# A graph layer with routed experts: 192 instead of 256 slots for each expert of the third group

## The chip, the cores and the metric

The kernel runs on one core of one Trainium2 chip, all in float32. The metric is the device time of a run in microseconds, the median of several runs; lower is better. Before the change it is 1236.64 us.

## The reference, cut to what matters

The input is 3,125 nodes of 256 features and 100,000 directed edges, sorted by their target. The layer adds a graph part and an attention part to the nodes, then a mixture of 8 experts of which each node uses its best two:

```python
xn = _layernorm(x, axis=-1)
x = x + gnn(xn, src, dst, theta, phi) + mix(xn[None], w_qkv, w_out, b_out)[0]
x = x + ffn(_layernorm(x)[None], Wr, br, ln_g, ln_b, W1, b1, W2, b2)[0]
...
# gnn: the largest message over a node's incoming edges
e = relu((x[dst] - x[src]) @ theta.T + x[src] @ phi.T)
out = segment_max(e, dst)
...
# ffn: E = 8 experts, D = 256, H = 1024
probs = softmax(xt @ Wr + br);  top_p, top_idx = top_k(probs, 2)
weights = top_p / top_p.sum(-1)
h = gelu(einsum('end,edh->enh', xn * ln_g + ln_b, W1) + b1)
y = einsum('enh,ehd->end', h, W2) + b2
out = sum over the two of weights * y[top_idx]
```

## The kernel before, in words

**Nodes and groups.** The nodes lie in 25 tiles of 128. Most edges end at the first nodes, so the edges are taken from the last target to the first, and the tiles in four groups as their edges are done: tiles 12 to 24, 6 to 11, 1 to 5, and tile 0 (`GROUPS`, line 41, with `STEPS`, line 42, the columns of 128 edges of each). What is left of the edges is handled apart.

**Edges.** GpSimd gathers one row of `b_d` for each of 128 edges per instruction (helper `gather`, line 106), into windows of 8 steps out of a pool of 5 buffers named `g`. VectorE folds each step into a running maximum (`fold`, line 365), SyncE's queue stores the windows to `s_d`. When a group's steps are folded, its tiles are routed (`token_tile`, lines 421 to 494): the last row of each node is gathered from `s_d`, joined with what other lanes carried over, normalized, and the router's two best experts are taken.

**Slots.** In the first three groups each node's row is scattered by GpSimd into `xs_d`, which has a fixed number of slots for each expert: `CAPS`, line 43, is 512, 256 and 256 for the three groups. `slots` (line 518) counts the rows of each expert; if one has more rows than slots, a flag in `bad` sends the program into a general path at its end (line 1393).

**The experts of the three groups** run as a stream of lots (`Stream`, line 652). A lot is 256 rows of one expert; two lots (`two`, line 664) are loaded with one transfer on ScalarE's queue. `turn` (line 683) transposes a lot on TensorE, `scaled` (line 692) applies the expert's gain and bias on ScalarE. `Units.run` (line 606) then makes 8 steps. In each, line 613 multiplies 128 hidden columns of W1 (stationary) with the lot's rows (moving, 256 columns) in two halves, line 615 applies the gelu, and `second` (line 624) makes an eighth of the second layer of the lot *before*: at line 639 hT is the stationary operand, in parts of 128 rows, and W2's 256 columns move. `done` (line 738) adds the second bias with a matmul (line 740), copies the part to `ys` (line 741), and stores two lots at a time to `ys_d`. A float32 matmul is two instructions in the trace. The weights of an expert are 2 MB, in three buffers, loaded in parts on ScalarE's queue between the steps.

**Tile 0**, the last, is not scattered: all its rows go through all 8 experts (`dense_tile`, line 773), in the order of `DENSE` (line 35), with the same `Units` at 128 rows. It starts with three experts' weights left by the stream; the others are loaded during it, one of them by `dense_half` (line 1181) into two buffers of the pool `g` (line 1310) after the routing of tile 0 (`clock["shared"]`, line 1136).

**Combining.** `combine` (line 1277) gathers each node's two rows from `ys_d`, weights and adds them on VectorE (line 1290), and stores tiles to `out` on SyncE's queue. These start after the last edge gather; the sums wait for `shared`.

**What orders the work.** TensorE, VectorE, ScalarE and SyncE run in an order written out by the program: tasks are generators that yield a number of ticks (`start`, `tick`, lines 1049 to 1066). A tick stands for 1.25 us (`TICK`, line 57), and each gather or scatter on GpSimd moves the clock on by one. `on_pe` (line 78) charges TensorE work to a second clock, and `room` (line 648) makes the stream yield until that clock is no more than two ticks ahead; so the charges decide how many steps of the experts are put between other work. In the dense layer a step yields one tick, and it doesn't start before the stream is through (line 792, set at line 764).

Of the kernel before, what the change touches and what calls it, by code (L numbers as in the profile page):

```python
# [13 lines left out]
AF = mybir.ActivationFunctionType  # L14
# [5 lines left out]
P = 128  # L20
# [4 lines left out]
D = 256  # L25
# [5 lines left out]
E = 8  # L31
H = 1024
FC = H // P
# [6 lines left out]

GROUPS = ((12, 25), (6, 12), (1, 6), (0, 1))
STEPS = (240, 161, 228, 126)
CAPS = (512, 256, 256)
G = len(GROUPS)
COL = [sum(STEPS[:g]) for g in range(G + 1)]

# [11 lines left out]
ROWS = 256  # L58
# [8 lines left out]
def gps_layer(ctx: ExitStack, tc: tile.TileContext, x, src, dst, thetaT, phiT, gbias, wq, wkvT,  # L67
              woT, bout, wr, br, small, w12, b2, out):
    nc = tc.nc
# [8 lines left out]
    def on_pe(us):  # L78
        clock["pe"] = max(clock["pe"], clock["now"]) + us / TICK
# [46 lines left out]
    ident = keep.tile([P, P], F32, name="ident")  # L126
# [472 lines left out]
    class Units:  # L599

        def __init__(self, ps, act, n, whole=False):
            self.ps, self.act, self.n, self.behind, self.whole = ps, act, n, None, whole

        def run(self, e, w1t, xe, w2t, done, between):

            n = self.n
            hT = []
            for f in range(FC):  # L610
                hp = self.ps.tile([P, ROWS], F32, name="hp")
                for c in range(2):
                    nc.tensor.matmul(hp[:, 0:n], w1t[:, c, f, :], xe[:, c, 0:n], start=(c == 0), stop=(c == 1))  # L613
                hT.append(self.act.tile([P, ROWS], F32, name="hT", bufs=14))
                nc.scalar.activation(hT[f][:, 0:n], hp[:, 0:n], AF.Gelu, bias=sm[:, 4 + f, e:e + 1])  # L615
                on_pe(n / P * 0.43)
                self.second(f)
                if f in between:
                    between[f]()
                yield  # L620
            self.second(FC)
            self.behind = [hT, w2t, done, {}]

        def second(self, f):

            if self.behind is None:
                return
            hT, w2t, done, yp = self.behind
            ns = self.n // P
            per = FC * ns // FC  # L630
            if f and f * per % FC == 0:
                done(f * per // FC - 1, yp[f * per // FC - 1])
            if f == FC:
                return
            for k in range(f * per, (f + 1) * per):
                r, q = k // FC, k % FC
                if q == 0:
                    yp[r] = self.ps.tile([P, D], F32, name="yp")
                nc.tensor.matmul(yp[r], hT[q][:, r * P:(r + 1) * P], w2t[:, q, :], start=(q == 0),  # L639
                                 stop=(q == FC - 1 and self.whole))  # L640
            on_pe(per * 0.43)

# [9 lines left out]
    class Stream:  # L652
# [18 lines left out]
        def at(self, to):  # L671

            return xn_hi[:, 4 * to:4 * to + 4, :]

        def as_two(self, rows, v):
            return rows.rearrange("p (k s) d -> p k s d", k=1 if CAPS[self.lots[2 * v][0]] == 2 * ROWS else 2)

        def rows(self, v):
            if 2 * v < len(self.lots) and ("xs", v) not in self.held:
# [3 lines left out]
        def turn(self, u):  # L683
            if ("xs", u // 2) in self.held and ("tr", u) not in self.held:
                tr = self.held["tr", u] = self.ps.tile([P, 2, ROWS], F32, name="trf", bufs=1)
                for c in range(2):
                    for r in range(ROWS // P):
                        nc.tensor.transpose(tr[:, c, r * P:(r + 1) * P],  # L688
                                            self.held["xs", u // 2][:, u % 2 * 2 + r, c * P:(c + 1) * P], ident)
                on_pe(ROWS / P * 0.6)  # L690

        def scaled(self, u):
            if ("tr", u) in self.held and ("xe", u) not in self.held:
                e = self.lots[u][1]
                xe = self.held["xe", u] = self.act.tile([P, 2, ROWS], F32, name="xe")
                for c in range(2):
                    nc.scalar.activation(xe[:, c, :], self.held["tr", u][:, c, :], AF.Identity,
                                         bias=sm[:, 2 + c, e:e + 1], scale=sm[:, c, e:e + 1])

        def next_w(self, q, parts=None):  # L700
# [5 lines left out]
                self.parts.pop(0)()  # L706

        def go(self):
            units = Units(self.ps, self.act, ROWS)
            u, q = 0, -1  # L710
            for k in range(3):
                self.next_w(k)
                yield 25
            while True:
                if u == len(self.lots):

                    for _ in units.last():
                        yield room()
                    units.behind = None
                    if not self.open:  # L720
                        break
# [12 lines left out]
                v = u // 2  # L734
                if u % 2 == 0:
                    ys = self.at(2) if v % 2 else self.act.tile([P, 4, D], F32, name="ys", bufs=1)

                def done(r, yp, u=u, ys=ys):
                    g, e, h = self.lots[u]
                    nc.tensor.matmul(yp, ident[0:E, e:e + 1].to_broadcast([E, P]), b2_sb, start=False, stop=True)  # L740
# [17 lines left out]
                for _ in units.run(e, w1t, self.held["xe", u], w2t, done, between):  # L758
# [14 lines left out]
    def dense_tile(act, ps, mm, i, shared, w, next_w, order=range(E), ready=None):  # L773
# [7 lines left out]
        held = {}  # L781
# [28 lines left out]
        units = Units(ps, act, P, True)  # L810
        for k, e in enumerate(order):
            def done(r, yp, k=k, e=e):
                if k == 0:
                    nc.vector.tensor_scalar(o, yp, full[:, e:e + 1], None, op0=OP.mult)
                else:
                    nc.vector.scalar_tensor_tensor(o, yp, full[:, e:e + 1], o, op0=OP.mult, op1=OP.add)

            between = {1: lambda k=k: scaled(k + 1)}
            if k == 1:
                between.update({3: second_bias, 5: add_bias})  # L820
            if k > 1:
                between[1] = lambda k=k: (next_w(k - 2), scaled(k + 1))
            while k == 1 and not shared:
                yield 1
            for _ in units.run(e, w[e][0], held["xe", e], w[e][1], done, between):
                yield 1
        nc.vector.tensor_add(o, o, x_sb[:, i, :])
        for _ in units.last():
# [49 lines left out]
    def loads():  # L878
# [664 lines left out]
```

## Time and profile before

| | |
|---|---|
| median of 3 runs | 1236.64 us (1230.59 to 1245.63) |
| the profiled execution's own time | 1752.15 us |
| its span, first to last instruction | 1750.4 us |
| TensorE matmul busy | 1035.4 us |
| VectorE busy | 670.9 us |
| ScalarE busy | 330.2 us |
| GpSimd busy | 881.0 us |
| mean granted TensorE clock | 0.756 of full |
| moved by DMA | 322.09 MB |

The profiled execution is 515.5 us longer than the median of the runs. A profile line of a group gives its line, engine, operation, tiles and count, then its busy time with the mean duration of one, then the idle time of the engine ahead of it and what ended that. In order of time, a line gives its start and duration in us, engine, line and count. "PEld" is TensorE's weight load. Matmul durations overlap, so that the distance of their starts is their pace. In the table by stretches each engine has its busy time and its count of instructions; the last columns are the granted TensorE clock, the share in which the 16 DMA engines were busy, and what they moved.

### The profile page before, as it was taken

What the parts mean: (1) busy time and instruction counts of PE and PEld (TensorE: products, weight loads), DVE (VectorE), ACT (ScalarE), POOL (GpSimd) and SP (SyncE); (2) the same over time, 40 slices, a digit from 0 to 9 for tenths busy, and PEclk for the clock granted to TensorE, in tenths of its full rate; (3) what the DMA queues carried; (4) which work ended last, traced back from release to release, by engine and by line L of the source; (5) the groups of instructions that cost most, each with busy time, mean ns of one, the idle gap of its engine ahead of it and who ended that gap; (6) DMA issues with size and microseconds to landing.
All of it is one profiled execution on the core that took longest, in us unless ns stands there. A gap on an engine that the chain in (4) does not pass through costs nothing.

```text
span 1750.4 us, 13366 instructions
## 1 busy us (share of the span) xinstructions
PE 1035.4 (59%) x3931; PEld 726.5 (42%) x3931; DVE 670.9 (38%) x1989; ACT 330.2 (19%) x763; POOL 881.0 (50%) x911
## 2 busy tenths in 40 slices
PE   3633654533653574169678735669677424299886
PEld 2412322321222332048556623457456213178675
DVE  3635554674254532310046440251253453013332
ACT  1301121110121211013123201213122111032232
POOL 6374757557556437723541573552462747723332
PEclk7866877866675577569887866889889556599998
DMA  7454756556465226416554563566687438468282
GB/s 230 133 160 158 235 198 199 192 189 220 146 234 186 107 92 215 151 53 219 183 173 154 188 206 99 181 230 235 229 276 248 148 136 285 122 207 298 69 288 89
DMA packets 105292, 322.09 MB, mean 184 GB/s; under 512 B 20982, under 2 KB 44911, under 8 KB 93690
## 3 DMA queue, kind: packets, MB, share of 16 engines
q0 software_dynamic: 44032, 119.73, 22.7%
q1 hardware_dynamic: 29740, 115.08, 16.9%
q10 hardware_dynamic: 31438, 86.33, 14.9%
q8 instruction: 33, 0.54, 0.1%
q14 instruction: 49, 0.40, 0.1%
HBM read 192.71 MB, written 128.36 MB: 183 GB/s over the span
## 4 chain that ended last, share of the span: by engine, by line
PE 40%; another core or an unknown queue 25%; issue 17%; DVE 11%; ACT 3%; DMA 3%; POOL 1%; ACTq 0%; DVEq 0%; SPq 0%; POOLq 0%
PE hp L613 15%; PE yp L639 13%; DVE g L365 4%; PE yp L740 2%; PE mm L402 2%; PE kv L998 1%; PE bp L240 1%; PE mm L400 1%; ACT hT L615 1%; POOL g L106 1%; PE trf L688 1%; DMA g<-b_d,srcI 1%; ACT sq L1002 1%; DVE r L449 1%
## 5 line engine op out<-in xcount | busy, mean ns | idle before, releaser
L106 POOL DMA_INDIRECT g<-b_d,srcI x755 | 733.9, 972 | 531.7 <-DMA s_d<-g 224.1
L613 PE MATMUL hp<-xe,w 128*128 128x256 f32 (+1 forms) x1216 | 334.1, 403 | 288.1 <-issue 180.4
L365 DVE SCALAR_TENSOR_TENSOR g<-g,cut 128x256 f32<-128x256 f32 x751 | 362.4, 483 | 247.0 <-DMA g<-b_d,srcI 146.2
L613 PEld LDWEIGHTS hp<-xe,w 128*128 128x128 f32 x1216 | 236.1, 210 | 349.2 <-issue 201.5
L639 PE MATMUL yp<-w,hT 128*128 128x256 f32 x1120 | 313.7, 405 | 0.0
L615 ACT ACTIVATE hT<-hp,sm 128x256 f32<-128x256 f32 (+1 forms) x320 | 143.7, 452 | 672.0 <-PE hp L613 274.8
L639 PEld LDWEIGHTS yp<-w,hT 128*128 128x128 f32 x1120 | 221.5, 203 | 43.5 <-issue 12.6
L1213 DVE SCALAR_TENSOR_TENSOR xn_lo<-xn_lo,no_edge 128x256 f32<-128x256 f32 x96 | 46.0, 480 | 194.9 <-DMA xn_lo<-b_d 178.2
L998 PE MATMUL kv<-wkv,xn_lo 128*128 128x512 f32 x96 | 61.0, 795 | 89.9 <-DVE kn L1016 39.7
L998 PE MATMUL kv<-wkv,xn_hi 128*128 128x512 f32 x104 | 59.7, 727 | 65.9 <-DVE kn L1016 37.1
L106 POOL DMA_INDIRECT g<-ys_d,from_i x48 | 45.5, 947 | 73.1 <-DMA out<-g 46.2
L106 POOL DMA_INDIRECT r<-s_d,end_i x25 | 24.1, 964 | 101.8 <-DMA s_d<-g 63.0
L998 PEld LDWEIGHTS kv<-wkv,xn_lo 128*128 128x128 f32 x96 | 23.5, 257 | 119.3 <-issue 99.4
L400 PE MATMUL mm<-bias,ones 1*128 1x512 f32 x50 | 36.0, 807 | 60.9 <-ACT x_sb L407 47.1
L998 PEld LDWEIGHTS kv<-wkv,xn_hi 128*128 128x128 f32 x104 | 23.3, 236 | 93.4 <-issue 91.2
L113 POOL DMA_INDIRECT xs_d<-xn_lo,slot_i x22 | 22.6, 1027 | 73.4 <-issue 62.6
L444 PE MATMUL am<-cr,oh 128*128 128x257 f32 x88 | 38.4, 567 | 29.2 <-DVE r L449 15.8
L113 POOL DMA_INDIRECT xs_d<-xn_hi,slot_i x26 | 27.3, 1050 | 50.4 <-issue 50.1
L1007 DVE TENSOR_REDUCE var<-sq 128x16 f32<-128x1024 f32 x25 | 30.4, 1215 | 47.3 <-ACT sq L1002 25.3
L740 PE MATMUL yp<-b_sb,ident 8*128 8x256 f32 x128 | 46.5, 444 | 0.0
L488 PE MATMUL mm<-br_sb,ones 1*128 1x8 f32 x50 | 12.9, 329 | 55.8 <-issue 37.6
L1002 ACT ACTIVATE sq<-kv 128x1024 f32<-128x1024 f32 x25 | 25.5, 1019 | 103.6 <-PE kv L998 44.6
(285 smaller groups left out, 999.6 us busy)
## 6 DMA issues: line engine op xcount, KB each, us to landing
s_d<-g SPq DMA_DIRECT2D x80, 1024.0 KB
w<-in_w ACTq DMA_DIRECT2D x84, 512.0 KB
w<-in_w ACTq DMA_DIRECT2D x6, 2048.0 KB
g<-b_d,srcI POOLq DMA_INDIRECT x755
s_d<-g SPq DMA_DIRECT2D x13, 896.0 KB
xn_hi<-xs_d ACTq DMA_DIRECT2D x16, 512.0 KB
xs_d<-zero ACTq DMA_DIRECT2D x8, 512.0 KB
xs_d<-zero ACTq DMA_DIRECT2D x16, 256.0 KB
```

The source lines that it names most:

```text
L106: got = nc.gpsimd.indirect_dma_start(out=to, out_offset=None, in_=table, in_offset=row_index(index))
L113: put.append(nc.gpsimd.indirect_dma_start(out=table, out_offset=row_index(index), in_=of, in_offset=None))
L365: nc.vector.scalar_tensor_tensor(g[:, j, :], last, cut[:, t:t + 1], g[:, j, :], op0=OP.add, op1=OP.max)
L400: nc.tensor.matmul(am, ones[0:1, :], bias, start=True, stop=False)
L444: nc.tensor.matmul(r2, picks[k], carried[g], start=(k == 0), stop=(k == len(slices) - 1))
L613: nc.tensor.matmul(hp[:, 0:n], w1t[:, c, f, :], xe[:, c, 0:n], start=(c == 0), stop=(c == 1))
L615: nc.scalar.activation(hT[f][:, 0:n], hp[:, 0:n], AF.Gelu, bias=sm[:, 4 + f, e:e + 1])
L639: nc.tensor.matmul(yp[r], hT[q][:, r * P:(r + 1) * P], w2t[:, q, :], start=(q == 0), stop=(q == FC - 1 and self.whole))
L740: nc.tensor.matmul(yp, ident[0:E, e:e + 1].to_broadcast([E, P]), b2_sb, start=False, stop=True)
L998: nc.tensor.matmul(kv[:, k, :], xnT(i, c), wkv[:, c, k * INNER:(k + 1) * INNER], start=(c == 0), stop=(c == 1))
L1002: nc.scalar.activation(sq, kv.rearrange("p k (h e) -> p (k h) e", e=DH), AF.Square)
L1213: nc.vector.scalar_tensor_tensor(of_k[:, k, :], b, no_edge[:, k, i:i + 1], of_k[:, k, :], op0=OP.add, op1=OP.max)
```

## The change

The third group gets 192 slots for each expert, and its lots have 192 rows in two parts of 96 instead of two of 128. For that, `Units` takes the number of parts and their rows with each run, and the transfers, transposes, scalings, bias matmuls and copies of a lot cover the rows that it has. A pair of lots of the third group lies on 96 partitions. The lots of the other groups, and tile 0, have the rows that they had.

```diff
-CAPS = (512, 256, 256)
+CAPS = (512, 256, 192)
+LOT = (256, 256, 192)
...
-        def run(self, e, w1t, xe, w2t, done, between):
-
-            n = self.n
+        def run(self, e, w1t, xe, w2t, done, between, parts, part):
+
+
+            n = parts * part
             hT = []
             for f in range(FC):
                 hp = self.ps.tile([P, ROWS], F32, name="hp")
...
-            self.behind = [hT, w2t, done, {}]
+            self.behind = [hT, w2t, done, {}, parts, part]
...
-            hT, w2t, done, yp = self.behind
-            ns = self.n // P
-            per = FC * ns // FC
+            hT, w2t, done, yp, per, part = self.behind
...
-                nc.tensor.matmul(yp[r], hT[q][:, r * P:(r + 1) * P], w2t[:, q, :], start=(q == 0),
+                nc.tensor.matmul(yp[r][0:part, :], hT[q][:, r * part:(r + 1) * part], w2t[:, q, :], start=(q == 0),
                                  stop=(q == FC - 1 and self.whole))
...
-            self.lots += [(g, e, h) for e in range(E) for h in range(CAPS[g] // ROWS)]
+            self.lots += [(g, e, h) for e in range(E) for h in range(CAPS[g] // LOT[g])]
+
+        def half(self, u):
+
+            return LOT[self.lots[u][0]] // 2
...
-            one = CAPS[g] == 2 * ROWS
-            rows = what[g][e * CAPS[g]:e * CAPS[g] + 2 * ROWS]
-            return rows.rearrange("(k p s) d -> p k s d", p=P, k=1 if one else 2)
+            rows = what[g][e * CAPS[g]:e * CAPS[g] + 2 * LOT[g]]
+            return rows.rearrange("(k p s) d -> p k s d", p=LOT[g] // 2, k=2 * LOT[g] // CAPS[g])
...
-                    for r in range(ROWS // P):
-                        nc.tensor.transpose(tr[:, c, r * P:(r + 1) * P],
-                                            self.held["xs", u // 2][:, u % 2 * 2 + r, c * P:(c + 1) * P], ident)
-                on_pe(ROWS / P * 0.6)
+                    for r in range(2):
+                        nc.tensor.transpose(tr[:, c, r * n:(r + 1) * n],
+                                            self.held["xs", u // 2][0:n, u % 2 * 2 + r, c * P:(c + 1) * P],
+                                            ident[0:n, 0:n])
+                on_pe(1.2)
...
-                    nc.scalar.activation(xe[:, c, :], self.held["tr", u][:, c, :], AF.Identity,
+                    n = 2 * self.half(u)
+                    nc.scalar.activation(xe[:, c, 0:n], self.held["tr", u][:, c, 0:n], AF.Identity,
                                          bias=sm[:, 2 + c, e:e + 1], scale=sm[:, c, e:e + 1])
...
-                    nc.tensor.matmul(yp, ident[0:E, e:e + 1].to_broadcast([E, P]), b2_sb, start=False, stop=True)
-                    nc.scalar.copy(ys[:, u % 2 * 2 + r, :], yp)
+                    n = self.half(u)
+                    nc.tensor.matmul(yp[0:n, :], ident[0:E, e:e + 1].to_broadcast([E, n]), b2_sb, start=False, stop=True)
+                    nc.scalar.copy(ys[0:n, u % 2 * 2 + r, :], yp[0:n, :])
...
-            fill = xs_d[g][0:E * cap].rearrange("(e p t) d -> e p t d", p=P, e=E)
+            n = LOT[g] // 2
+            fill = xs_d[g][0:E * cap].rearrange("(e p t) d -> e p t d", p=n, e=E)
...
-                move(nc.scalar, fill[e], zero.to_broadcast([P, cap // P, D]))
+                move(nc.scalar, fill[e], zero[0:n].to_broadcast([n, cap // n, D]))
```

More of the change, by code (lines that the diff above doesn't have):

```diff
@@ L599, in gps_layer, with __init__ @@
     class Units:
-        def __init__(self, ps, act, n, whole=False):
-            self.ps, self.act, self.n, self.behind, self.whole = ps, act, n, None, whole
-        def run(self, e, w1t, xe, w2t, done, between):
-            n = self.n
+        def __init__(self, ps, act, whole=False):
+            self.ps, self.act, self.behind, self.whole = ps, act, None, whole
+        def run(self, e, w1t, xe, w2t, done, between, parts, part):
+            n = parts * part
             hT = []
@@ L675, in as_two @@
         def as_two(self, rows, v):
-            return rows.rearrange("p (k s) d -> p k s d", k=1 if CAPS[self.lots[2 * v][0]] == 2 * ROWS else 2)
+            g = self.lots[2 * v][0]
+            return rows[0:LOT[g] // 2].rearrange("p (k s) d -> p k s d", k=2 * LOT[g] // CAPS[g])
         def rows(self, v):
@@ L708, in go @@
         def go(self):
-            units = Units(self.ps, self.act, ROWS)
+            units = Units(self.ps, self.act)
             u, q = 0, -1
@@ L739, in done @@
                     g, e, h = self.lots[u]
-                    nc.tensor.matmul(yp, ident[0:E, e:e + 1].to_broadcast([E, P]), b2_sb, start=False, stop=True)
-                    nc.scalar.copy(ys[:, u % 2 * 2 + r, :], yp)
+                    n = self.half(u)
+                    nc.tensor.matmul(yp[0:n, :], ident[0:E, e:e + 1].to_broadcast([E, n]), b2_sb, start=False, stop=True)
+                    nc.scalar.copy(ys[0:n, u % 2 * 2 + r, :], yp[0:n, :])
                     if u % 2 and r:
@@ L757, in go @@
                 w1t, w2t = self.held["w", q]
-                for _ in units.run(e, w1t, self.held["xe", u], w2t, done, between):
+                for _ in units.run(e, w1t, self.held["xe", u], w2t, done, between, 2, self.half(u)):
                     yield room()
@@ L808, in add_bias @@
             nc.vector.tensor_add(x_sb[:, i, :], x_sb[:, i, :], bb)
-        units = Units(ps, act, P, True)
+        units = Units(ps, act, True)
         for k, e in enumerate(order):
@@ L824, in dense_tile @@
                 yield 1
-            for _ in units.run(e, w[e][0], held["xe", e], w[e][1], done, between):
+            for _ in units.run(e, w[e][0], held["xe", e], w[e][1], done, between, 1, P):
                 yield 1
```

## The prediction, made before the changed kernel ran

> **What bounds the kernel now.** First the page, whose gathers and matrix groups are the two large items; then busy time by stretch, for the part of the program that the third group's experts can touch; then the chain that ended last; then the order of time on TensorE.
>
> ```profile
> L106 POOL DMA_INDIRECT g<-b_d,srcI x755 | 733.9, 972 | 531.7 <-DMA s_d<-g 224.1
> ...
> L613 PE MATMUL hp<-xe,w 128*128 128x256 f32 (+1 forms) x1216 | 334.1, 403 | 288.1 <-issue 180.4
> ...
> L639 PE MATMUL yp<-w,hT 128*128 128x256 f32 x1120 | 313.7, 405 | 0.0
> ```
>
> The edge gathers fill GpSimd: each is busy 0.95 us and followed by 0.30 us of issue, 1.25 us in all (that is the kernel's TICK). The profiled execution took 1752.15 us and the unprofiled runs 1236.64, so 516 us of its waits don't exist in an ordinary run. A check on what does: the first gather is at 70.99 us of the trace, and stepping the kernel's own planner (`clock["now"]`) to its end gives 931 ticks; 71 + 931 x 1.25 = 1235 us. So the ordinary run keeps about the plan's pace, and I read places from the plan and prices from the trace.
>
> Next, TensorE, VectorE, ScalarE and GpSimd in three stretches: from the third group's last scatter, from when TensorE stops waiting, and from the start of tile 0's dense layer.
>
> ```profile
> core 0: us, PE busy (x) PEld busy (x) DVE busy (x) ACT busy (x) POOL busy (x), PEclk, DMA share, GB/s
> 1435.00:1537.00 102.00, 34.03 (x94) 24.38 (x94) 20.58 (x46) 8.89 (x17) 70.98 (x74) 0.58 0.60 199
> 1537.00:1664.00 127.00, 118.81 (x531) 95.75 (x529) 40.05 (x119) 36.55 (x83) 37.20 (x39) 0.96 0.60 200
> 1664.00:1743.00 79.00, 65.95 (x389) 58.52 (x387) 22.90 (x56) 23.65 (x65) 22.69 (x24) 0.89 0.59 202
> ```
>
> In the middle one TensorE is busy 118.81 of 127 us, while nothing else reaches 41. The chain of waits runs through it; from the third group's last expert:
>
> ```profile
> 1653.35 0.97 PE hp L613 x4
> ...
> 1655.80 3.65 PE yp L639 x16
> ...
> 1660.08 3.65 PE yp L639 x16
> 1663.73 0.64 PE yp L740 x2
> ...
> 1665.21 0.64 ACTq L99
> ...
> 1666.32 1.16 PE hp L613 x8
> ```
>
> So the third group's experts end at 1664.3, and tile 0's dense layer begins behind them on TensorE, 14 us after its input was there (L778's transpose is at 1650.4). The dense layer's last sum is at 1743, its store starts at 1743.10, the span ends at 1750.4. In this tail a microsecond of the experts' TensorE time is a microsecond of the run.
>
> Prices, in order of time on TensorE, full clock:
>
> ```profile
> 1594.49 1.03 PE L613 MATMUL hp<-xe,w 128*128 128x256 f32 x4
> 1595.36 1.03 PE L639 MATMUL yp<-w,hT 128*128 128x256 f32 x4
> 1596.22 1.03 PE L613 MATMUL hp<-xe,w 128*128 128x256 f32 x4
> ...
> 1699.94 0.61 PE L613 MATMUL hp<-xe,g 128*128 128x128 f32 x4
> 1700.38 0.60 PE L639 MATMUL yp<-xn_hi,hT 128*128 128x256 f32 x2
> 1700.82 0.61 PE L613 MATMUL hp<-xe,g 128*128 128x128 f32 x4
> ```
>
> Starts, not durations, give the pace, since these overlap. Four instructions of 256 columns take 0.86 us (1594.49 to 1595.36), 0.215 each. In the dense layer four of 128 columns take 0.44 (1699.94 to 1700.38), 0.11 each.
>
> **What the Trainium skill says.** "TensorE: Matmul & The Clock Gate", section "Back-to-back issue gap": the gap grows with the moving columns, N / 2.4 ns plus a constant, and its section "LDWEIGHTS (loading the stationary operand)" has the load's price go by the stationary operand's columns. The trace agrees in kind: 0.215 against 0.11 us for 256 against 128 columns. The stationary operand of L613 stays 128 wide, and its load kept up at 0.11 us an instruction in the dense layer, so it doesn't bind at 0.16. "DMA: Bandwidth & Descriptors", section "Why a DMA increments its semaphore by 16 and not by 1", says that a tile of 96 partitions spreads over 16 engines like one of 128; no transfer of the kernel before has 96, so the trace neither shows nor denies it.
>
> **The change, part by part.**
>
> *Does it hold the tokens?* A slot count too small would set `bad` and start the general path. Counting the two best experts of tokens 128 to 767 with the reference's own inputs gives 148 to 178 for an expert: under 192. That risk is out.
>
> *L613, first layer.* 8 experts x 8 steps x 4 instructions = 256, each from 256 to 192 columns. On the line between the two prices: 0.11 + 0.105 / 2 = 0.163 us, saving 0.052. 256 x 0.052 = 13.2 us. Bounds: nothing if the weight load set the pace (excluded above), 13.2 if it goes by columns.
>
> *L639, second layer.* It streams 256 columns of the weights through a stationary hT, now 96 wide: the same 256 instructions of 0.215 us. Nothing, and this is half of TensorE's work. The bias matmul at L740 also streams 256 columns: nothing.
>
> *L688, transposes.* 4 of 0.15 us busy per expert stream fewer columns; 32 x 0.15 x 1/4 = 1.2 us at most, I take 0.5.
>
> *ScalarE.* L615 is 0.47 us at 256 columns, 0.37 at 128, so some 0.42: 64 x 0.05 = 3.2 us saved, worth nothing, since ScalarE is busy 36.55 of 127 us. With L613 shorter a step is 0.65 + 0.86 = 1.51 us instead of 1.72; the activation and its DMA issue still fit.
>
> *Transfers.* Four loads and four stores of 512 KB become 384 KB: 1 MB less of some 45 MB (229 us from 1435 to 1664 at 200 GB/s). Fewer zero rows in the early fill, beside the gathers. Nothing. If a 96-partition transfer were no faster or twice as slow: the first load takes 4.0 us (1438.90 to 1442.96) with TensorE waiting, so at worst +4; the three others are issued most of two experts ahead.
>
> *Order of work.* `on_pe` charges a step 0.645 instead of 0.86 us for L613: 64 x 0.215 / 1.25 = 11.0 ticks less. Stepping the planner: the third group's experts begin at tick 756, the last gather is at 828, tile 0's transposed rows at 845, its routing is done (`shared`) at 854, the experts are through and the dense layer starts at 858. The last becomes 847. Everything else keeps its tick. So the dense layer still finds its input emitted ahead of it (845), with 2 ticks to spare: the cover is used up exactly. The dense layer's second expert waits for `shared` at 854, but its first takes 8 ticks, to 855.
>
> What now stands behind what: tile 0's router matmuls (L488, L490) come behind some of the dense layer's first matmuls instead of behind L613 and L639 of the last expert, of the same length; ScalarE's last copies to ys come ahead of the router's copy, both soon after the same TensorE work. On VectorE the dense layer's scalings (L789) move 11 ticks forward past the combining sums (L1290). In the trace the seventh of them sat behind sums that waited for their gathers, and TensorE idled 5.28 us at 1717.53; with the scalings ahead part of that may go, and the sums' chain ends later relative to the dense layer. It ended at 1729.0 with the last out store near, against 1743.1: 14 us of slack, which the saving nearly uses up.
>
> Sum: 13.2 + 0.5 = 13.7 us at full clock, and the planner's shift, 11.0 ticks x 1.25 = 13.75, agrees. Against the profiled execution's own time: in it 56 of the 256 L613 instructions run in the stretch with TensorE waiting (102 us, 34.03 busy; ScalarE's idle there is put down to nothing known), so only 200 x 0.052 + 0.5 = 10.9 us of its 1752.15 are certain. Those waits mostly don't exist in an ordinary run, which has no room for them, so I take 13.6 there: 1236.64 - 13.6 = 1223.0 us, 1.1% less. A difference of 1% (12.4 us) is about what a measurement of this kernel can tell from none.
>
> **Rivals.**
>
> *A: the whole of it on the path* (above): 11 to 16 us, 1221 to 1226. For it: 118.81 of 127 us and the chain. Chance 0.58.
>
> *B: the experts are fed, not computed, while gathers run.* In an ordinary run they overlap the gathers for (828 - 756) x 1.25 = 90 us. Gathers of 128 KB per 1.25 us and stores as much are 210 GB/s, 2 MB of weights per 16 us 131 more, rows some 30: 371 GB/s, and faster experts ask for 390. If the transfers limit that part, only what is left at the last gather speeds up: 30 ticks, 38 us, 2.4 experts x 1.7 = 4 us, to 9 with part of the rest: 1228 to 1233. Against it: slices with 400 GB/s and more are in the trace. Chance 0.20.
>
> *C: another chain ends last.* The sums and stores, or tile 0's own path (last fold, r gather, router), don't shorten. With their slack as said, the gain is 0 to 8: 1229 to 1237. Chance 0.09.
>
> *D: slower.* One mechanism: the dense layer's fifth expert needs weights whose load is issued after `shared` (L1310, L1181), which doesn't move, while their use moves 14 us forward. In the trace the load is issued at 1663.62 and first read at 1699.06, 35 us later; 2 MB at 200 GB/s take 10. It costs only if the load takes over 35 - 14 = 21 us, and beats the saving from 35 us on; with TensorE's clock falling in the wait, 1240 to 1252. Behind a TensorE that waits there stand the second layers of that expert and all that follows. Chance 0.13.
>
> **How the numbers follow.** Likeliest is A at 1223.0. Beyond 1% (a gain over 12.4 us) lie 0.47 of A's 0.58 and 0.03 of the others: 0.50. Within: 0.11 of A, 0.18 of B, 0.08 of C: 0.37. Slower: D's 0.13. The range, with a tenth left out at each end, is 1214 (the 5 us stall gone as well, with a spread of the runs of half a per cent) to 1241 (into D); A's own is 1217 to 1228.
>
> **What would show it.** L613 of the third group as 128x192 with starts 0.65 us apart per four: right, 0.86: wrong. L639 still 0.86. From the first L688 of the group to the dense layer's first L613, 11 to 14 us less where TensorE doesn't wait. The chain should still go L639, L740, dense L613; if it goes through L1290 and out stores, C; if the dense layer's hp<-xe,g waits for a transfer, D. The prediction is wrong if TensorE now idles between the expert steps.

## The result, and the profile after

| | before | after |
|---|---|---|
| median | 1239.66 us (20 runs, 1230.59 to 1245.63) | 1229.45 us (20 runs, 1224.61 to 1235.91) |
| ratio, with its 95% interval | | 0.9917 (0.9897 to 0.9937) |
| span of an ordinary profiled execution | 1237.3 us | 1225.8 us |

The change takes 10.2 us (0.8%) off, 8 to 13 by the interval, where 13.6 were forecast. So the time lies in the range (1214 to 1241), but not in that of rival A (1221 to 1226), which had the greatest chance; it lies where B (1228 to 1233) and C (1229 to 1237) had put it.

The execution behind the prediction was 42% longer than an unprofiled run. The kernel before was therefore profiled once more; that execution ("before again", 1239.11 us) is an ordinary one and is what the comparisons below use. Beside some experiments ("long runs" below) every execution, of the kernel before too, took 1724 to 1794 us, with stalls of some 20 us on TensorE and ScalarE whose releaser the records mostly don't name, so those are compared only with the kernel before of the same time, and their traces are read only where no such stall lies.

The page of the changed kernel first, for the groups shown of before: line, engine, operation, tiles and count, then busy time and mean of one, then idle time ahead. L107 is the old L106, L615 the old L613.

```profile
L107 POOL DMA_INDIRECT g<-b_d,srcI x755 | 739.4, 979 | 237.3 <-issue 203.2
...
L639 PE MATMUL yp<-w,hT 128*128 128x256 f32 (+1 forms) x1120 | 295.4, 386 | 5.3 <-DVE o L824 5.3
L615 PE MATMUL hp<-xe,w 128*128 128x256 f32 (+2 forms) x1216 | 285.2, 361 | 4.5 <-issue 1.7
```

L615 is 285.2 us; in the ordinary execution of before, its L613 was 300.0. L639 now idles 5.3 us for an `o` of VectorE, where before it idled for nothing.

Then the busy time by stretches: from the third group's first transposes to the dense layer's first matmul, and from there to the end. Before again:

```profile
core 0: us, PE busy (x) PEld busy (x) DVE busy (x) ACT busy (x) POOL busy (x), PEclk, DMA share, GB/s
1014.93:1157.98 143.05, 139.80 (x624) 112.09 (x624) 60.58 (x162) 45.88 (x100) 103.86 (x107) 0.97 0.83 302
1157.98:1237.30 79.32, 62.40 (x388) 56.12 (x387) 22.69 (x55) 23.76 (x65) 22.70 (x24) 0.91 0.59 207
```

And the changed kernel:

```profile
1010.67:1143.93 133.26, 125.66 (x617) 98.95 (x617) 51.26 (x132) 41.85 (x100) 98.75 (x102) 0.96 0.86 314
1143.93:1225.80 81.87, 65.46 (x393) 59.33 (x393) 31.92 (x86) 23.60 (x65) 28.00 (x30) 0.88 0.57 205
```

TensorE's work in the first stretch fell by 14.1 us (139.80 to 125.66), as forecast, but the stretch only by 9.8: TensorE's idle time in it went from 3.3 to 7.6 us. The second stretch grew by 2.5. Together the two are 7.2 shorter. The first transposes themselves stand 4.3 us earlier in this trace; over the five ordinary traces of kernels that don't differ ahead of that place but for the third group's slots they stand from 1010.67 to 1020.75, so I count this as scatter of single executions.

The hand-over from the experts to tile 0's dense layer is where the first part goes. TensorE in order of time, before again (start, duration, engine, line, count, in brackets the idle time ahead):

```profile
1144.08 0.38 PE L778 MATMUL mm<-ident,xn_lo 128*128 128x128 f32 x2
...
1157.36 0.69 PE L740 MATMUL yp<-b_sb,ident 8*128 8x256 f32 x2
1157.98 1.16 PE L613 MATMUL hp<-xe,w 128*128 128x128 f32 x8
```

The changed kernel, the same place:

```profile
1139.28 0.67 PE L748 MATMUL yp<-b_sb,ident 8*96 8x256 f32 x2
1141.92 0.69 PE L482 MATMUL mm<-ident,xt 128*128 128x128 f32 x2 [1.98 <-ACT xt L471]
1142.40 0.63 PE L786 MATMUL mm<-ident,xn_lo 128*128 128x128 f32 x2
1143.93 2.08 PE L615 MATMUL hp<-xe,w 128*128 128x128 f32 x8 [0.90 <-DVE xe L797]
```

Before, tile 0's transposes (L481, L778) lay 13.9 us ahead of the dense layer, among the experts' steps, and the dense layer followed the last bias matmul (L740) in 0.62 us. Now they come behind the last bias matmul (L748), TensorE waits 1.98 us ahead of them and 0.90 us behind, and the dense layer follows in 4.65 us, at half pace at first (8 instructions in 2.08 us instead of 1.16).

What the wait of 1.98 us stands on, from ScalarE's order of time in the changed kernel:

```profile
1139.98 0.37 ACT L749 COPY xn_hi<-yp 96x256 f32<-96x256 f32 x1 [3.85 <-PE yp L748]
...
1140.75 0.46 ACTq L100 DMA_DIRECT2D xn_hi<-in_w  x1
1141.27 0.60 ACT L471 ACTIVATE xt<-x_sb,off,root 128x256 f32<-128x256 f32 x1 [0.92 <-DVE xn_lo L221]
```

The activation that makes `xt` is written behind the last expert's last copy and two DMA issues (the store of `ys_d` at 1140.38 is the one left out), and starts when they are out, 1.3 us after the copy began. The bracket names VectorE's `xn_lo`, which this activation doesn't read; its last operand `off` was ready on VectorE at 1140.36, so by its operands it could have started 0.9 us earlier. The rest of the wait is tile 0's normalization on VectorE, which ends behind the last bias matmul.

The end of the program is the second part. The chain of waits of the changed kernel, its last stretch (the first line shown is a row gather, then a sum, an addition of the dense layer, and its matmuls):

```profile
1173.51 16.30 DMA g<-ys_d,from_i
...
1210.84 0.48 DVE g L1299
1211.33 0.41 DVE o L824
1211.78 6.29 PE yp L639 x16
```

From 1151 us on it no longer runs through the dense layer's steps, but through the row gathers of the sums and VectorE, and comes back to TensorE at 1211.78: the sum at L1299 waits for its gathered rows, `o` (L824), which frees a buffer of TensorE's, stands behind it in VectorE's order, TensorE idles 5.3 us and then takes 6.3 us for sixteen instructions that take 3.7 when it has not waited. Before, the end lost about as much in this way, in front of L613 at 1209.87 (5.52 us idle).

### The profile page after: what moved, and what is told of

Same layout as the page of the kernel before. It is cut to its first block, busy times and chain, and to the rows that moved or that the text cites. A ratio compares the mean times of both kernels' runs of the same rounds, so it can differ in the third digit from the quotient of the medians.

```text
span 1225.8 us, 13367 instructions
## 1 busy us (share of the span) xinstructions
PE 936.1 (76%) x3931; PEld 671.4 (55%) x3931; DVE 677.0 (55%) x1989; ACT 326.9 (27%) x763; POOL 886.6 (72%) x911
## 4 chain that ended last, share of the span: by engine, by line
PE 39%; DMA 23%; POOL 16%; issue 10%; DVE 10%; ACT 1%; ACTq 0%; POOLq 0%; DVEq 0%; SPq 0%
DMA g<-b_d,srcI 18%; POOL g L107 15%; PE yp L639 15%; PE hp L615 14%; DVE g L366 4%; DMA g<-ys_d,from_i 3%; PE yp L748 3%; PE bp L241 2%; PE mm L403 2%; DMA r<-s_d,end_i 1%; PE mm L401 1%; PE trf L693 1%; POOL xs_d L114 1%; PE tr L234 1%; PE am L445 0%
## 5 line engine op out<-in xcount | busy, mean ns | idle before, releaser
L107 POOL DMA_INDIRECT g<-b_d,srcI x755 | 739.4, 979 | 237.3 <-issue 203.2
L639 PE MATMUL yp<-w,hT 128*128 128x256 f32 (+1 forms) x1120 | 295.4, 386 | 5.3 <-DVE o L824 5.3
L615 PE MATMUL hp<-xe,w 128*128 128x256 f32 (+2 forms) x1216 | 285.2, 361 | 4.5 <-issue 1.7
L615 PEld LDWEIGHTS hp<-xe,w 128*128 128x128 f32 x1216 | 217.2, 195 | 39.8 <-issue 11.9
L617 ACT ACTIVATE hT<-hp,sm 128x256 f32<-128x256 f32 (+2 forms) x320 | 141.2, 441 | 326.2 <-PE hp L615 325.3
L639 PEld LDWEIGHTS yp<-w,hT 128*128 128x128 f32 (+1 forms) x1120 | 202.1, 186 | 44.3 <-issue 11.5
L107 POOL DMA_INDIRECT g<-ys_d,from_i x48 | 45.8, 955 | 42.5 <-DVE g L1299 14.8
L445 PE MATMUL am<-cr,oh 128*128 128x257 f32 x88 | 38.9, 574 | 33.6 <-DVE r L450 26.3
L445 PEld LDWEIGHTS am<-cr,oh 128*128 128x128 f32 x88 | 21.7, 277 | 42.6 <-issue 32.7
L748 PE MATMUL yp<-b_sb,ident 8*128 8x256 f32 (+1 forms) x128 | 43.9, 422 | 0.0
L704 ACT ACTIVATE xe<-trf,sm 128x256 f32<-128x256 f32 (+1 forms) x64 | 31.6, 547 | 24.0 <-PE trf L693 24.0
L1030 PEld LDWEIGHTS dots_p<-kn,vn 128*128 128x128 f32 x200 | 26.7, 197 | 19.1 <-issue 17.5
L1030 PE MATMUL dots_p<-kn,vn 128*128 128x128 f32 x200 | 27.6, 282 | 9.0 <-DVE kn L1025 9.0
```

The source lines that it names most:

```text
L107: got = nc.gpsimd.indirect_dma_start(out=to, out_offset=None, in_=table, in_offset=row_index(index))
L445: nc.tensor.matmul(r2, picks[k], carried[g], start=(k == 0), stop=(k == len(slices) - 1))
L639: nc.tensor.matmul(yp[r][0:part, :], hT[q][:, r * part:(r + 1) * part], w2t[:, q, :], start=(q == 0), stop=(q == FC - 1 and self.whole))
L704: nc.scalar.activation(xe[:, c, 0:n], self.held["tr", u][:, c, 0:n], AF.Identity, bias=sm[:, 2 + c, e:e + 1], scale=sm[:, c, e:e + 1])
L748: nc.tensor.matmul(yp[0:n, :], ident[0:E, e:e + 1].to_broadcast([E, n]), b2_sb, start=False, stop=True)
L1030: nc.tensor.matmul(dots_p[:, r, :], vn[:, r * P:(r + 1) * P], knf[:, r * P:(r + 1) * P], start=(i == 0 and r == 0), stop=(i == NT - 1), sk ...
```

## The experiments

Beside the ordinary runs the kernel before had a median of 1238.17 us (47 runs), beside the long ones 1758.98 to 1768.44.

**The kernel before, once more.** No edit.

> The kernel before, unchanged, for a second profile, since the first one lasted 1752 us and the changed kernel's 1226. Theory (TensorE's work on the path, then two covers used up): the span is near 1238; the third group's experts take some 140 us from their first transpose to their last bias matmul on TensorE, and the dense layer starts within 2 us behind them, after its input. Rival (the experts are fed by transfers): TensorE shows waits inside the experts' steps before the last edge gather.

Measured: span 1237.3 us, clock 0.859 (0.756 in the execution of the prediction); shown above. The dense layer follows the experts in 0.62 us, and the only waits inside the experts' stretch are 2.3 us for folds on VectorE and 0.8 us for ScalarE, none for a transfer.

**The work alone.** The changed kernel, with the experts' first layer charged in the list of due times (the plan in ticks) as for 256 rows, so that the order stays as before.

```diff
-                on_pe(n / P * 0.43)
+                on_pe(parts * 0.43)
```

> The changed kernel, but the planner charges a step of the third group as for 256 rows, so that the order of all engines is that of the kernel before. Theory: TensorE is behind its plan through the whole tail, so most of the shorter matmuls arrive even in the old order: 5 to 10 us under before, 1230 to 1235. If it is the order that gains (rival): 0 to 2 us under before, 1238 to 1240.

Measured: 1237.02 us, ratio to before 0.9982 (0.9957 to 1.0008). A miss: nearly all of the gain is gone. The stretch from first transposes to dense layer tells where; TensorE's work did fall:

```profile
1013.40:1153.69 140.29, 129.09 (x623) 102.65 (x623) 60.82 (x162) 41.41 (x100) 104.07 (x107) 0.93 0.84 301
```

Busy fell by 10.7 us (139.80 to 129.09), the stretch by 2.8 (143.05 to 140.29). TensorE idles inside of the order, for instance here:

```profile
1060.71 0.48 PE L1255 MATMUL mm<-ident,end_f 128*128 128x128 f32 x1 [4.21 <-DVE run_at L1252]
1060.98 1.49 PE L615 MATMUL hp<-xe,w 128*128 128x192 f32 x4
1062.26 1.91 PE L639 MATMUL yp<-w,hT 128*96 128x256 f32 x4
```

A matmul of tile 0's preparation (L1255, of `last_ends`) is placed for slower experts; TensorE comes to it 4.2 us before VectorE does, waits, and then runs at half pace (1.28 us from L615 to L639 instead of 0.65). Here the work saved under an unchanged order became waits. This execution was a quick one of its kernel (1231.81 us), and shows only part of the loss: from the first transposes to the end it takes 216.6 us, against 222.4 before and 215.1 in the changed kernel.

**The order alone.** 256 slots and rows as before, the third group charged as for 192.

```diff
-CAPS = (512, 256, 192)
-LOT = (256, 256, 192)
+CAPS = (512, 256, 256)
+LOT = (256, 256, 256)
...
-                on_pe(n / P * 0.43)
+                on_pe((n - self.less) / P * 0.43)
...
+                units.less = 64 if g == 2 else 0
```

> 256 slots and lots of 256 rows as in the kernel before, but the planner charges the third group's steps as for 192 rows: the order of the changed kernel with the work of before. Theory (work on TensorE's path): the experts end when they did before, so within 3 us of before, 1237 to 1243. If the order is the gain (rival): 8 to 10 us under before, 1230 to 1232.

Measured: 1238.3 us, ratio 1.0011 (0.9989 to 1.0032): nothing. So neither half of the change carries the gain; they do it together (the rival of the work alone had the right number, 0 to 2 us, for the wrong reason). This trace also shows that the new order alone moves tile 0's transposes behind the experts:

```profile
1152.53 0.69 PE L482 MATMUL mm<-ident,xt 128*128 128x128 f32 x2 [2.05 <-ACT xt L471]
...
1154.54 2.08 PE L616 MATMUL hp<-xe,w 128*128 128x128 f32 x8 [0.90 <-DVE xe L799]
```

The last bias matmul starts at 1149.79, 4.75 us ahead of the dense layer, with the experts' work unreduced: the wait comes of the order. The time is as it was expected (1237 to 1243).

**The sums later on VectorE.** The changed kernel, with the third group's sums (L1299) 20 ticks later in the list of due times.

```diff
-        yield 10
+        yield 10 if g < 2 else 30
```

> The changed kernel with the third group's combining sums put 20 ticks later in VectorE's order, so that the dense layer's last additions no longer stand behind sums that wait for their gathers (TensorE idles 5.32 us at 1211.78 for that, and its next 16 instructions take 6.28 instead of 3.7 us). Theory: 4 to 8 us under the changed kernel, 1221 to 1226. If the sums and their stores end the run anyway (rival): the same as the changed kernel within 2 us, or a few us slower.

Measured: 1224.45 us, ratio 0.9915 (0.9885 to 0.9945). That can't be told from the changed kernel (0.9917), although in the trace the wait is gone. TensorE's waits from 1140 us on, the longest two of four (total, times, longest):

```profile
PE mm L482 <- ACT xt L471: 2.0, 1, 2.0
PE mm L815 <- DVE bt L810: 1.6, 1, 1.6
```

The 5.3 us for `o` are missing, and the dense layer to the end takes 76.0 us instead of 81.9. TensorE's last matmuls start at 1215.54, and now the stores of the sums, issued at 1221.98 on SyncE's queue, come last. So the wait can be removed, at the price of sums that end last. From the first transposes to the end this trace has 209.5 us, against 215.1 in the changed kernel, but its transposes stand 10 us later; the gain in the median is not settled.

It was repeated beside the unaltered changed kernel, in long runs.

> The changed kernel itself, unaltered, timed beside the next three so that they can be compared with it under the same conditions. Expected: about 10 us under the kernel before (1228 to 1231), with the same 4 us between the third group's last bias matmul and the dense layer's first matmul as in the first profile of the changed kernel (1139.28 to 1143.93), and the same idle TensorE before the last dense expert.

> The changed kernel with the third group's sums on VectorE (L1299) taken up 20 ticks later in the list of due times, so that the scalings of the dense layer (L797) don't stand behind sums that wait for gathered rows; it was timed once (1224.45, 0.9915 of before), and is repeated beside the changed kernel. If part of the saving is given back at the end because VectorE stands in sums that wait for gathers: 3 to 6 us under the changed kernel. If the end is set by TensorE or the gathers themselves: within 1 us of it.

Measured: 1753.98 us for the changed kernel (ratio 0.9974, 0.9887 to 1.006), 1767.24 with the later sums (0.9969, 0.9849 to 1.0089). Inconclusive for the time of both. The hand-over isn't touched by the stalls of the long runs: in the changed kernel L748 at 1660.80, the dense layer at 1665.00, with the same waits of 1.97 and 0.90 us.

**Still less work in the experts.** First layer of the third group with half of its sum left out in five of eight steps, the charge cut accordingly.

```diff
-                for c in range(2):
+                k = 1 if n == 192 and f in (0, 2, 3, 5, 6) else 2
+                for c in range(k):
...
-                on_pe(n / P * 0.43)
+                on_pe(n / P * 0.215 * k)
```

> The changed kernel with still less TensorE work in the third group's experts: in five of the eight steps of the first layer the second half of the sum over the model's width is left out (so the product of those steps is computed on half of the input), which takes 80 of the 256 instructions of L615 with 192 columns away, 13 us by their 0.163 us each; the charges in the list of due times fall with it. Theory, that tile 0's own path (its softmax, transposes, copies and scaling on ScalarE and VectorE, and the sequence in front of them) now sets when the dense layer can start: the last bias matmul of the third group comes 10 us or more earlier, the dense layer's first matmul at most 4 us earlier, and the whole is 0 to 4 us under the changed kernel. Rival, that TensorE's work in the experts still sets it: the dense layer starts 10 to 13 us earlier and the whole is 8 to 13 us shorter.

> As the run before it with this edit, which fell into a call where every run, of the kernel before too, took 1740 to 1790 us: the changed kernel without the second half of the first layer's sum in five of its eight steps of the third group (80 of 256 instructions of L615 with 192 columns, 13 us by 0.163 us each; the output is then computed from half of the input in those steps). Theory, that tile 0's own path now sets the dense layer's start: the last bias matmul 10 us or more earlier after the third group's first transposes than in the changed kernel (128.61), the first dense matmul at most 4 us earlier (133.26), and 1225 to 1229. Rival, that the experts' work still sets it: the dense layer starts 10 us or more earlier, and 1216 to 1221.

> The same edit a third time, in the hope of an ordinary call (the two before took 1720 to 1790 us for every kernel): the second half of the first layer's sum left out in five of its eight steps for the third group, so 80 of 256 instructions of L615 with 192 columns, 13 us by 0.163 us each; the output is then computed from half of the input in those steps. Theory, that tile 0's own path now sets the dense layer's start: the last bias matmul comes 10 us or more earlier after the third group's first transposes than in the changed kernel (128.61), the first dense matmul at most 4 us earlier (133.26), and the time is 1225 to 1229. Rival, that the experts' work still sets it: the dense layer starts 10 us or more earlier, and 1216 to 1221.

Measured, all three in long runs: 1738.43 us (0.987, 0.9781 to 0.9959), 1751.42 (0.9814, 0.9746 to 0.9881), 1758.57 beside 1768.44 (too few runs for an interval). With the changed kernel itself at 0.9974 (0.9887 to 1.006), its time is unclear. The hand-over of the first of them on TensorE:

```profile
1654.25 0.67 PE L749 MATMUL yp<-b_sb,ident 8*96 8x256 f32 x2
...
1655.81 0.70 PE L445 MATMUL am<-cr,oh 128*128 128x257 f32 x2 [0.52 <-DVE cr L389]
1662.37 0.69 PE L482 MATMUL mm<-ident,xt 128*128 128x128 f32 x2 [5.86 <-DVE xn_lo L221]
...
1664.38 2.08 PE L616 MATMUL hp<-xe,w 128*128 128x128 f32 x8 [0.90 <-DVE xe L798]
```

With the experts through sooner, even tile 0's carry (L384, L445: what other lanes carried over joins its rows) comes behind them, and the wait for its normalized rows, first transposed at L482, is 5.86 us, in the other two traces 6.00 and 5.87. From the last bias matmul to the dense layer it is 10.1 to 10.3 us in the three, 4.65 in the changed kernel. From the carry's last matmul (1655.81) the dense layer is 8.6 us away by tile 0's path alone, 5.7 of them a row of 23 VectorE instructions from 1656.54 to 1662.20. So the place is shown: once the experts are through, the dense layer waits for tile 0's path. How much earlier it starts is not. The two numbers that were expected after the first transposes can't be read from these traces, since stalls lie in between (in the first of them ScalarE stands still for 11.6 us until 1650.93, just ahead of the carry). The times speak rather for the rival, 1738.43 against 1753.98 us for the changed kernel of the same time, though the intervals overlap; the theory's 0 to 4 us are not confirmed.

**A charge between the two.** The changed kernel, with the third group's first layer charged as for 208 rows, 3 ticks more.

```diff
-                on_pe(n / P * 0.43)
+                on_pe((208 if n == 192 else n) / P * 0.43)
```

> The changed kernel with its work as it is, but with the first layer of the third group charged in the list of due times as if it had 208 rows and not 192, so that the dense layer comes some 3 ticks later in the instruction order. Theory, that TensorE reaches the dense layer 4 us before its input is there: steps of the last experts fill this wait, the wait before the first dense matmul falls below 2 us, and the time is 0 to 3 us under the changed kernel. Rival, that the order has no such slack: the same 3 to 4 us later start of the dense layer and a time 1 to 4 us above.

> The changed kernel with the third group's first layer charged as if it had 208 rows, in an ordinary call. Theory, that TensorE reaches the dense layer 4 us before its input is there: the wait between the last bias matmul and the first dense matmul (4.65 in the changed kernel) falls below 2 us, and the time is 1225 to 1229. Rival, that the order has no such slack: the dense layer starts 3 to 4 us later and the time is 1230 to 1234.

Measured, in long runs: 1749.1 us (0.9916, 0.9822 to 1.001) and 1750.76 (0.9885, 0.9848 to 0.9921). The hand-over of the first:

```profile
1668.45 0.44 PE L482 MATMUL mm<-ident,xt 128*128 128x128 f32 x2 [0.42 <-ACT xt L471]
1668.72 1.03 PE L639 MATMUL yp<-w,hT 128*96 128x256 f32 x4
...
1670.76 0.67 PE L748 MATMUL yp<-b_sb,ident 8*96 8x256 f32 x2
...
1671.95 5.44 PE L615 MATMUL hp<-xe,w 128*128 128x128 f32 x36
```

The mechanism is as the theory has it: tile 0's transposes and router lie among the last expert's steps again, the wait is 0.42 instead of 1.97 us, the dense layer follows the last bias matmul in 1.19 us, at the pace it had before (36 instructions in 5.44 us, 28 in 4.22 before). The forecast times don't apply to long runs, and the intervals overlap that of the changed kernel: whether 2 or 3 us are won in the whole was not settled.

**Both mends together.**

> Both mends together: the third group's first layer charged as if it had 208 rows, so that steps of the last experts fill the wait before the dense layer, and the sums of the third group on VectorE 20 ticks later. Theory, that the part of the saving that didn't arrive was lost in these two places: the wait ahead of tile 0's transposes 0.4 us instead of 2, the dense layer's first matmul under 2 us behind the last bias matmul (4.65 in the changed kernel), no wait of TensorE before the last dense expert for a VectorE that stands in sums, and 1219 to 1224 (0.984 to 0.989 of before; in a call where all is longer, the same difference). Rival, that the end is set by the gathers and stores of the sums: 1225 to 1230 (0.990 to 0.993), with stores of out as the last thing in the chain.

Measured, in long runs: 1761.29 us, ratio 1.0047 (1.0007 to 1.0087). A miss: no faster than the kernel before, though the hand-over shows what was expected (L482 waits 0.42 us, the dense layer 1.18 us behind the last bias matmul). From there on TensorE still waits 12.0 us in five places ahead of L615, with no releaser named, so what it lost isn't known. No version was shown to beat the changed kernel.

## Why the prediction was right and wrong

**TensorE bounds the experts: right, to the size.** From the third group's first transposes to its last bias matmul it was 142.43 us (1014.93 to 1157.36) and is 128.61 (1010.67 to 1139.28): 13.8 less, 13.7 predicted. That the whole stretch fits so closely is luck in part: TensorE's busy time in it fell by 15.3 us (139.18 to 123.88), since tile 0's transposes and router moved behind it, and its idle time rose by 1.5. The price of an instruction is the firmer evidence. TensorE in the changed kernel, one step after the other:

```profile
1021.76 0.81 PE L615 MATMUL hp<-xe,w 128*128 128x192 f32 x4
1022.41 1.03 PE L639 MATMUL yp<-w,hT 128*96 128x256 f32 x4
```

Four of 192 columns take 0.65 us (0.163 each, as interpolated), and four of L639 still 0.86 (the next L615 starts at 1023.27). The rule of "TensorE: Matmul & The Clock Gate", section "Back-to-back issue gap", that the gap grows with the moving columns, held between the two sizes, and the weight load didn't bind. The size of the gap is another: by the page's formula 256 columns would take an estimated 0.109 us, and an instruction here takes 0.215.

**What was costed at nothing: right.** The first load of 96 partitions took 3.62 us (1007.05 to 1010.67), of 128 partitions 3.92 (1011.01 to 1014.93). The experts of the changed kernel don't wait for transfers (rival B is out, though the time lies in its range: behind the first load TensorE waits for no transfer up to the hand-over, and 0.6 us at L615, for ScalarE), and no `hp<-xe,g` waits (rival D is out).

**The failed step: "the dense layer still finds its input emitted ahead of it (845), with 2 ticks to spare: the cover is used up exactly", costed at nothing.** It was worth 4.0 us at once, and more behind it: the prediction had asked for 11 to 14 us less from the first transposes to the dense layer, and it is 9.8. Emitted ahead in the list isn't there ahead in time. The check by which the plan's ticks had been taken for times (71 + 931 x 1.25 = 1235 us) came out by luck: 71 us is the first gather of the long execution. In the ordinary one it is at 48.15 us, so the plan would end at 1212 us, and tile 0's transposes (tick 845) come some 40 us behind their tick, the dense layer (858) some 37. The cover was counted as 14 us from tile 0's transposes to the dense layer, but the copy and the scalings behind the transposes take another 1.5 us (1142.40 to 1143.93), so only 12.4 us were free and 13.8 were taken: 1.4 us. The other 2.6 us come from the order: tile 0's transposes stand 129.15 us behind the group's first transposes before, and 131.73 after.

Tile 0's path isn't independent of the experts: its carry (L383, after the change L384) is a TensorE matmul in the same order. VectorE's copy of its result, before again, with the idle time in which VectorE waited for TensorE:

```profile
1134.17 0.42 DVE L388 COPY cr<-mm 128x256 f32<-128x256 f32 x1 [4.46 <-PE mm L383]
```

The changed kernel:

```profile
1133.87 0.42 DVE L389 COPY cr<-mm 128x256 f32<-128x256 f32 x1 [8.82 <-PE mm L384]
```

The carry's input was ready at nearly the same place, 114.8 and 114.4 us behind the group's first transposes, but TensorE came to it at 118.8 and 122.8, with more of the experts' steps ahead of it. The same wait is 5.24 us in the work-alone run, which has the old order, and 8.97 in the order-alone run, so it goes with the order and not with the work. VectorE's normalized rows of tile 0 then end 3.0 us later (127.2 and 130.2), and `xt` stands behind the last copy and two DMA issues on ScalarE. I had even named that queue ("ScalarE's last copies to ys come ahead of the router's copy") and given it no price. No run moves the carry forward in TensorE's order, which might remove the wait without giving experts' steps back. The order-alone run has the same wait, the 208-row charge nearly removes it, and less work lengthens it.

**The loss goes on behind the wait.** From the dense layer's first matmul to its first L639 it took 6.19 us before (1157.98 to 1164.17) and 9.02 after (1143.93 to 1152.95), since TensorE starts at half pace and the router's matmuls (L489, L491) now lie in it; to the first L613 or L615 behind the bias 5.66 and 7.36, with a wait of 1.63 us for `bt` (L810), which stands on VectorE behind the sums that begin when tile 0's router is done (L1299, from 1151.51 on). With the 208-row charge the first of these is 5.27, and the wait for `bt` 0.2.

**VectorE and the end: rival C, a part.** "with the scalings ahead part of that may go, and the sums' chain ends later": the stall didn't go, it moved from L613 (5.52 us) to L639 (5.32 us), behind `o` instead of the scalings, because the sums' slack was used up, as was said. The chain confirms C's sign (it runs through L1299 and the gathers). From the first L613 or L615 behind that bias to the end it is 67.47 and 65.49 us: 2.0 less.

The sum of these, against the two traces: -13.8 (experts) + 4.0 (wait for tile 0) + 2.8 + 1.7 (dense layer's start) - 2.0 (end) = -7.2 us with their second decimals, which is what the stretches show. The median says -10.2 (8 to 13). The 3 us between aren't explained; single executions scatter by as much, and the part of the program ahead of the third group differs by 4.3 us between these two.

**The weights of the rivals.** The sum of 13.6 us was right for the experts and was taken for the whole. A had 0.58 and C 0.09, which was too little for C: tile 0's own path stood in its text, with a cover that had just been computed as used up exactly. That the time lies in the range is owed to the range's width, which reached over A, B and C.

## What to carry to other kernels

Where an order written by a planner follows its charges, a saving of work pays only if the charge falls with it (the work alone gave 0.2%, the order alone nothing, both 0.8%); then look at what the earlier end is handed to. Cover that is "used up exactly" has to be counted to the arrival of the input, with every copy, scaling and DMA issue on its way, not to its place in the list. Where a link on that way runs on the very engine that was sped up (here the carry), it has its own place in that engine's order. A stretch that ends before its successor's input is there pays twice, in the wait and in TensorE's slower pace after it.

## What was unexpected of the hardware

TensorE's clock after short waits. "TensorE: Matmul & The Clock Gate", section "Part 1: The HAM clock gate (the "warmup" mystery)", says that the clock falls to half after an idle window of some 3.4 us. The traces agree on the half (sixteen L639 in 6.28 us after 5.32 us idle, where 3.69 are the rule), but no single wait had to be that long. The changed kernel, in stretches that end where its granted clock changed:

```profile
core 0: us, PE busy (x) PEld busy (x) DVE busy (x) ACT busy (x) POOL busy (x), PEclk, DMA share, GB/s
1118.00:1121.41 3.41, 1.85 (x8) 1.24 (x8) 1.35 (x5) 0.42 (x1) 1.84 (x2) 1.00 0.16 52
1121.41:1124.82 3.41, 3.41 (x10) 2.56 (x10) 1.38 (x4) 0.74 (x2) 2.50 (x4) 0.50 0.34 97
1138.48:1141.89 3.41, 1.46 (x7) 0.57 (x5) 2.05 (x13) 0.97 (x2) 2.60 (x3) 1.00 0.48 143
1141.89:1152.13 10.24, 9.31 (x40) 8.66 (x41) 3.68 (x19) 2.81 (x9) 6.64 (x7) 0.50 0.71 235
```

In the first and the third stretch, of 3.41 us each, TensorE was idle for 1.6 and 1.9 us in all, and at their ends the clock fell to half. The first fall came when TensorE had already been at work again for 1.9 us (from 1119.56), the second at the end of the first wait at the hand-over, so that the dense layer's first 8.2 us ran at half clock. The four places at which the clock changed lie 3.4, 17.1 and 10.2 us apart, whole multiples of 3.41. So it seems that the busy share of a window on a fixed grid decides, and not the length of one wait; that is read from this trace and not tested.
